# One-hots counted column by column, and the first node step and the lists between the pieces of the second sort, in a two-layer graph kernel

## The chip, the cores and the metric

The kernel runs on one core of a Trainium2 chip. The metric is the device time of one execution in microseconds (us). Eleven executions of the kernel before gave a median of 9892.93 us, from 9871.71 to 9947.75 us. Traces and profiles show a single execution. The engines are PE (matrix multiply), DVE (elementwise work), ACT (copies and functions), POOL (which issues the indirect transfers) and SP (which issues the plain transfers).

## The reference, cut to what matters

Two graph layers on 12,500 nodes of 128 features and 200,000 edges `src -> dst`. The first layer is a graph convolution with two sparse products, the second is attention with eight heads whose scores get a bias from a 128-wide attribute of every edge. Shortened:

```
mask = (src != dst); deg = segment_sum(mask, dst) + 1; dinv = deg ** -0.5
edge_w = dinv[src] * dinv[dst] * mask
spmm(h) = segment_sum(h[src] * edge_w, dst) + h / deg
h = spmm(relu(bn(spmm(x @ W1 + b1))) @ W2 + b2)
x = layernorm(x + h)
q, k, v = x @ q_w.T + q_b, x @ k_w.T + k_b, x @ v_w.T + v_b     # 8 heads of 16
scores = (q[src] . k[dst]) / 4 + edge_attr @ eb_w.T + eb_b
attn = softmax of scores over the edges of one src
x = layernorm(x + segment_sum(attn * v[dst], src) @ out_w.T + out_b)
```

The edges come in the order of `dst`. For the sparse products the kernel needs them grouped by pairs of blocks (128 nodes are a block, and there are 98), for the attention grouped by `src`. It makes both groupings on the chip.

## The kernel before

The edges lie as 128 partitions x 1563 columns. The work goes through these stages, and the change touches the first five of them.

**First sort, counts and records.** `load_raw` brings in `src` and `dst`. `keys_by_src` and `keys_by_blocks` make two sets of sort keys (128 x 2048). `bitonic` (L436) is a generator of 185 pieces (186 with the store behind it): compare-and-exchange steps on DVE (L460, L458 with a change of sign), and 14 times a turn of the whole array through PE and ACT (`turned`, L463 to L476), after which the generator yields 3. Beside the first sort, `counts` (L226) counts edges for each pair of blocks: for 16 columns at a time (`CW`) it writes three one-hots per edge (block of `dst`, block of `src`, row in the block: 98, 98 and 128 wide) with three DVE comparisons of the whole chunk (L234), each of two broadcast operands, and multiplies them on PE (L239, one matmul per column, summed in PSUM). It yields 2 after each of its 98 chunks. `woven` alternates the two generators and lets a yield of n hold its own generator back until the other has made n steps. `records` is a third generator, with 395 steps: it loads the edge attributes, turns them (PE L749, ACT L751), multiplies them by the bias weights (PE L764), and every eighth step turns the result back (ACT L777, PE L780) for DVE to add the bias (L782) and SP to store (L795) a table `rec` of records in DRAM. One of its steps, every third time two, follows each step of the weave.

**Decode of the first sort.** `windows_s` and `windows_a` find where each block begins. POOL gathers the sorted keys in tiles (`windowed`), and `decode_s` takes them apart on DVE: the edge numbers `idx_s`, rows, masks and gates for the attention, the last two with waits for their own stores and loads.

**Second sort and lists.** `beside` puts twelve pieces of the second sort (`sort_a`) under the first wait of `decode_s` and runs the rest of the second sort behind it. `chunks_b` is a generator of 83 steps (the lists `idx_b`, `loc_b`): 68 of them are eight DVE comparisons (L406, one per column of the list, 128 wide, with a per-partition scalar) and eight small matmuls (L408), and nine bring the results into form (L414 to L424). One step of it follows each piece of the sort from the 21st on. Then `decode_a` gathers and takes apart the second sort.

**The filler.** `placed` (L813) is a generator of 106 steps. A step has POOL gather one group of 16 x 128 records (16 indirect transfers, L809) through four buffers, and SP store the group that was gathered two steps earlier (L824). There are 104 groups, so the last two steps only store. The filler is stepped every eighth piece of the second sort beyond the 40th (19 times), every fourth step of the first node step (7), every 16th step of the first spread (31), every third step of the second node step (9) and every 16th step of the second spread (31). What is left of it runs out in a loop of its own before the second sum.

**First node step, then spread and sum.** `nodes_1` (L1079) loads `x`, turns it (PE L850, ACT L852), multiplies by W1 (PE L864) and writes `h_all` on DVE (`send`, L1076 and L1077), 25 groups in a pipeline. `spread` (488 tiles: one-hot on DVE L1007, four matmuls L1016, ACT L1020, store by SP L1025) writes a message per edge slot, and `summed` (544 tiles: gather by POOL, one-hot L1047, matmuls L1055, DVE L1061) adds them up by destination. `nodes_2`, a second spread and sum and `nodes_3` follow, and then attention and the output step, which the change leaves alone.

Each engine works through its own list in the order in which the generators above issued the work (the order is written by hand), so a generator that is stepped earlier moves all that it issues, on every engine and on SP and POOL too.

Of the kernel before, what the change touches and what calls it, by code (L numbers as in the profile page):

```python
# [1 line left out]

# [14 lines left out]
P = 128  # L17
# [3 lines left out]
G = 4  # L21
# [5 lines left out]
CW = 16  # L27
# [38 lines left out]


def beside(a, b):

    for n in a:  # L70
        yield
        for _ in range(n or 0):
            if next(b, StopIteration) is StopIteration:
                break
            yield
    yield from b
# [3 lines left out]
def kernel(  # L80
# [145 lines left out]
    def counts(pool, hi_s, hi_d, row_d):  # L226

        w = 2 * NB + P
        for c0 in range(0, EC, CW):
            n = min(CW, EC - c0)  # L230
            oh = pool.tile([P, CW, w], BF16, name="count_oh", bufs=3)
            k = 0
            for val, m in ((hi_d, NB), (hi_s, NB), (row_d, P)):
                nc.vector.tensor_tensor(  # L234
                    oh[:, :n, k:k + m], val[:, c0:c0 + n].unsqueeze(2).to_broadcast([P, n, m]),
                    iota_bf[:, :m].unsqueeze(1).to_broadcast([P, n, m]), op=ALU.is_equal)
                k += m
            for c in range(n):
                nc.tensor.matmul(pair_ps[:NB], oh[:, c, :NB], oh[:, c, NB:],  # L239
                                 start=(c0 + c == 0), stop=(c0 + c == EC - 1))  # L240
            yield 2
# [62 lines left out]
    def windows_s(pool, cnt):  # L304

        tiles, _, end = in_tiles(pool, cnt, 7, "s")
        pst = past(pool, end, NT, "past_s")
        by_j = pst.rearrange("b (p j) -> b j p", j=TPP)
        got = begins(pool, cnt, tiles, P, lambda j: by_j[:NB, j, :], TPP, pst, iota_w, "s")
        blk_i = pool.tile([1, NT], I32, tag="row", name="blk_i", bufs=1)  # L310
        tile_blocks(pst, NT, blk_i)
        nc.sync.dma_start(blk_sd, blk_i)
        return got
# [122 lines left out]
    def bitonic(pool, key, nm, out_):  # L436
# [42 lines left out]
        for k in range(1, LOGN + 1):  # L479
# [12 lines left out]
            else:  # L492
                key = turned(key, None)
                yield 3
# [4 lines left out]
                yield 3  # L499
# [35 lines left out]
    def sort_a(key):  # L535

        got = []
        yield from bitonic(keyp, key, "d", got)
# [3 lines left out]
    def decode_a(pool, begin):  # L542
# [6 lines left out]
        s_i = pool.tile([P, w], I32, tag="dec0", name="s_a", bufs=1)  # L549
        nc.vector.tensor_scalar(s_i, ff, 7, P - 1, op0=ALU.logical_shift_right,  # L550
                                op1=ALU.bitwise_and)
        seq = pool.tile([P, JA, R, P], BF16, tag="dec1", name="seq_at", bufs=1)
# [13 lines left out]
        drop = pool.tile([P, w], F32, tag="dec0", name="drop_a", bufs=1)  # L566
# [44 lines left out]
    def sort_s(key):  # L611

        got = []
        yield from bitonic(keyp, key, "s", got)
# [3 lines left out]
    def decode_s(pool, begin, blk):  # L618
# [12 lines left out]
        g = pool.tile([P, KC], I32, tag="dec0", name="g_s", bufs=1)[:NG]  # L631
        nc.vector.tensor_scalar(g, f, 31, None, op0=ALU.arith_shift_right)
        nc.vector.tensor_tensor(g, g, f, op=ALU.bitwise_xor)
        top = pool.tile([P, KC], F32, tag="dec1", name="top_s", bufs=1)[:NG]
# [10 lines left out]
        e_i = pool.tile([P, KC], I32, tag="dec1", name="e_i", bufs=1)[:NG]  # L645
# [6 lines left out]
        r_i = pool.tile([P, KC], I32, tag="dec1", name="r_i", bufs=1)[:NG]  # L652
# [4 lines left out]
        nd = pool.tile([P, TPP, P], F32, tag="dec0", name="nd", bufs=1)  # L657
# [4 lines left out]
        seq = pool.tile([P, KC], BF16, tag="dec1", name="seq", bufs=1)[:NG]  # L662
# [3 lines left out]
        loc_s = pool.tile([P, NT], F32, tag="row", name="loc_st", bufs=1)  # L666
# [194 lines left out]
    def times(psp, xt, n, w):  # L861
        mp = psp.tile([P, G, D], F32, tag="mp", name="n_mp", bufs=3)
# [30 lines left out]


    with ExitStack() as pre:
        ep = pre.enter_context(tc.tile_pool(name="edges", bufs=1))
        idx_s = ep.tile([P, NT], I32, name="idx_s")
        idx_b = ep.tile([P, NTB], I32, name="idx_b")
        loc_a = ep.tile([P, NTA, R], F32, name="loc_a")
        loc_b = ep.tile([P, NTB, R], F32, name="loc_b")  # L900
        blk_a = ep.tile([1, NTA], I32, name="blk_a")
        blk_b = ep.tile([1, NTB], I32, name="blk_b")
        filler = placed(ep)
        with tc.tile_pool(name="keys", bufs=1) as keyp, \
                tc.tile_pool(name="recs", bufs=1) as rp, \
                tc.tile_pool(name="pp", bufs=1, space=bass.MemoryType.PSUM) as pp:
            pair = rp.tile([P, 2 * NB], F32, name="pair", bufs=1)
            raw_d = load_raw(rp, dst, "d")
            table = records(rp)
            step(table)  # L910
            with tc.tile_pool(name="count", bufs=1) as pool:
                his = [pool.tile([P, EC], BF16, name=n_) for n_ in ("hi_s", "hi_d", "row_d")]
# [13 lines left out]
                pair_ps = pp.tile([P, NB + P], F32, tag="ps", name="pair_ps", bufs=2)  # L926
                with tc.tile_pool(name="count_oh", bufs=1) as pool:
                    sort = woven(counts(pool, *his), sort_s(key_s))
                    n = 0
                    while step(sort):  # L930
                        n += 1
                        step(table, 1 if n % 3 else 2)
            with tc.tile_pool(name="decode", bufs=1) as pool:

                nc.scalar.copy(pair[:NB, :NB], pair_ps[:NB, :NB])
                deg_r = pool.tile([P, P], F32, name="deg_r")
                nc.vector.tensor_scalar(deg_r[:NB], pair_ps[:NB, NB:], 1.0, None, op0=ALU.add)
                tp = pp.tile([P, NB], F32, tag="tp", name="pair_t", bufs=3)
                nc.tensor.transpose(tp[:NB], pair[:NB, :NB], ident[:NB, :NB])
                pair_t = pool.tile([P, NB], F32, name="pair_t")  # L940
                nc.vector.tensor_copy(pair_t[:NB], tp[:NB])
                cnt = pool.tile([P, 1], F32, name="cnt")[:NB]
                nc.vector.tensor_reduce(cnt, pair_t[:NB], AX.X, ALU.add)
                tp = pp.tile([P, NB], F32, tag="tp", name="deg_t", bufs=3)
                nc.tensor.transpose(tp, deg_r[:NB], ident[:NB, :NB])
                nc.scalar.activation(dinv, tp, AF.Sqrt)
                nc.vector.reciprocal(dinv, dinv)
                iota_t = pool.tile([P, NT], F32, name="iota_t")
                nc.gpsimd.iota(iota_t, pattern=[[1, NT]], base=0, channel_multiplier=0,  # L949
                               allow_small_or_imprecise_dtypes=True)  # L950
                iota_w = pool.tile([P, TPP], F32, name="iota_w")
                nc.gpsimd.iota(iota_w, pattern=[[P, TPP]], base=0, channel_multiplier=KC,
                               allow_small_or_imprecise_dtypes=True)
                iota_a = pool.tile([P, JA], F32, name="iota_a")
                nc.gpsimd.iota(iota_a, pattern=[[P, JA]], base=0, channel_multiplier=1,
                               allow_small_or_imprecise_dtypes=True)
                nc.vector.tensor_scalar(iota_a, iota_a, float(SA), None, op0=ALU.mult)
                sort = beside(decode_s(pool, *windows_s(pool, cnt)), sort_a(key_d))
                begin_a, first_a = windows_a(pool, cnt)
                lists = chunks_b(pool, pair[:, :NB], pair_t, first_a)  # L960
                early, n = 0, 0
                while step(sort):
                    n += 1
                    step(table, 2)
                    if n > 20:
                        step(lists)
                    if n % 8 == 0 and n > 40:
                        early += 1
                        step(filler)
                while step(lists):  # L970
                    pass
                for _ in decode_a(pool, begin_a):
                    pass
                while step(table):
                    pass

# [4 lines left out]

        h_all = wp.tile([P, NB, D], F32, name="h_all")
# [90 lines left out]
        def send(mp, bias, b, n):  # L1073

            o = h_all[:, b:b + n, :]
            nc.vector.tensor_add(o, mp[:, :n, :], wide(bias, n))  # L1076
            nc.vector.tensor_mul(o, o, tall(dinv[:, b:b + n], n))  # L1077

        def nodes_1():  # L1079
            a, c, e = {}, {}, {}  # L1080

            def s0(i):
                a[i] = load_x(pool, *groups[i])

            def s1(i):
                c[i] = transposed(pool, pp, a.pop(i), groups[i][1])

            def s2(i):
                e[i] = times(pp, c.pop(i), groups[i][1], w1_s)

            def s3(i):
                send(e.pop(i), b1_r, *groups[i])

            yield from pipeline(len(groups), s0, s1, s2, s3)

# [56 lines left out]
        with_records(nodes_1(), 4)  # L1152
        with_records(spread(msg1, D + 1), 16)
# [3 lines left out]
        with_records(spread(msg2, D), 16)  # L1157
# [43 lines left out]
    def attention(wp, psp):  # L1201
# [191 lines left out]
        chain = None  # L1393
        for s in range(NQ + ADD):
# [24 lines left out]
            for gen in bulk:  # L1419
                for _ in gen:  # L1420
                    left -= 1
                    if chain is not None and not step(chain):
                        chain = None
            if chain is not None and left > 0 and not step(chain, left):
                chain = None
            if 0 <= i < NQ and i % QN == QN - 1:
                chain = maxima(i // QN)
                step(chain)
# [89 lines left out]
```

## Time and profile before

| what | value |
|---|---|
| median of 11 executions | 9892.93 us |
| the profiled execution's own time | 9889.83 us |
| its span, first to last instruction | 9888.0 us |
| mean granted PE clock | 0.747 |
| busy share PE, DVE, ACT, POOL | 62%, 58%, 21%, 45% |

Stages, as the first and last instruction of their lines bound them:

| stage | from, us | to, us |
|---|---|---|
| first sort, counts, records | 66 | 1215 |
| windows, decode of the first sort | 1215 | 1412 |
| second sort with lists | 1412 | 1980 |
| decode of the second sort | 1980 | 2012 |
| first node step | 2012 | 2195 |
| first spread, first sum | 2195 | 4242 |
| second node step | 4242 | 4553 |
| second spread | 4553 | 5711 |
| rest of the filler, start of the second sum | 5711 | 5868 |

In a group of instructions the profile gives the line, engine, operation, tile written and tiles read, shapes and count, and after the bars the busy time with the mean of one, and the idle time of the engine before them with what ended it. "issue" and "remote" stand for a wait whose releaser the profile does not know. A timeline row gives start, duration, engine, line and tiles, and in brackets the idle time before it; rows of one kind are drawn together with a count.

### The profile page before, as it was taken

The page shows a single profiled execution, that of the slowest core. Times are in us where ns is not written, and L with a number is a line of the kernel's source. Part 1 is how long each engine was busy: PE and PEld are TensorE (multiplying, and loading weights), DVE is VectorE, ACT ScalarE, POOL GpSimd, SP SyncE. Part 2 cuts the span into 40 slices and gives each one's busy share as a digit, 9 for nine tenths or more (in the row PEclk, how much of TensorE's full clock was granted, in tenths as well). Part 3 has the DMA queues.
Part 4 walks back from the last instruction along what each step waited for, and adds up shares of the span by engine and source line. Part 5 has one row for each costly group of instructions (what it writes and reads, how often), then busy time and mean ns, then how long its engine had stood idle before and what let it go on. Part 6 is the DMA issues. An engine that isn't in the chain of part 4 may idle for free.

```text
span 9888.0 us, 117573 instructions
## 1 busy us (share of the span) xinstructions
PE 6131.8 (62%) x32059; PEld 4692.6 (47%) x32059; DVE 5686.5 (58%) x11412; ACT 2077.8 (21%) x5494; POOL 4497.4 (45%) x4450
## 2 busy tenths in 40 slices
PE   5777713137666777716767637772566676766665
PEld 2444412125555577615555526662455555555554
DVE  8888769723223466624323325557566666666667
ACT  1222200002222200002222200001233333333332
POOL 0000068263333366672433367760556565565651
PEclk9998855557777799956777769996666766676765
DMA  3333320013333466712333336673333333333343
GB/s 86 93 91 91 96 71 6 2 44 112 113 109 112 137 179 178 174 21 74 117 108 115 115 77 178 178 168 106 119 107 108 110 108 110 107 108 110 108 108 73
DMA packets 570541, 1045.40 MB, mean 106 GB/s; under 512 B 131594, under 2 KB 294678, under 8 KB 557252
## 3 DMA queue, kind: packets, MB, share of 16 engines
q0 software_dynamic: 220992, 514.28, 21.0%
q1 hardware_dynamic: 348928, 523.60, 16.0%
q8 instruction: 297, 4.87, 0.2%
q14 instruction: 324, 2.65, 0.1%
HBM read 722.51 MB, written 314.96 MB: 105 GB/s over the span
## 4 chain that ended last, share of the span: by engine, by line
PE 32%; DVE 12%; another core or an unknown queue 11%; issue 11%; POOL 4%; DMA 2%; DVEq 1%; ACT 1%; ACTq 0%; POOLq 0%; SPq 0%
PE ps L1055 12%; PE ex L1016 9%; POOL kvg L809 3%; PE qe L1259 3%; PE bc L1002 3%; PE ps L1379 2%; DVE acc L1381 2%; DVE kvg L1358 1%; DVE kvg L1269 1%; DMA got<-msg,idx_b 1%; DMA kvg<-kv,rec_in 1%; PE n_mp L864 1%; DVEq L889 1%; DVE oht L1248 1%
## 5 line engine op out<-in xcount | busy, mean ns | idle before, releaser
L809 POOL DMA_INDIRECT placed<-rec,idx_s x1664 | 1717.9, 1032 | 1838.2 <-DMA rec_s<-placed 1304.5
L809 POOL DMA_INDIRECT kvg<-kv,rec_in x1664 | 1636.9, 984 | 1391.3 <-PE ps L1379 574.9
L1016 PE MATMUL ex<-h_all,oht 128*128 x7808 | 1353.7, 326 | 731.4 <-DVE oht L1007 464.2
L1007 DVE TENSOR_SCALAR oht<-bc,iota_col 128x512 f32<-128x512 f32 x976 | 722.9, 750 | 1656.6 <-remote 805.1
L1016 PEld LDWEIGHTS ex<-h_all,oht 128*128 128x128 f32 x7808 | 1150.5, 226 | 1004.5 <-issue 687.4
L1055 PE MATMUL ps<-got,oh 128*128 128x128 f32 x8704 | 1232.1, 299 | 564.2 <-DVE acc L1061 275.8
L1055 PEld LDWEIGHTS ps<-got,oh 128*128 128x128 f32 x8704 | 1125.2, 207 | 671.1 <-DVE acc L1061 332.0
L809 POOL DMA_INDIRECT got<-msg,idx_b x1088 | 1115.9, 1026 | 559.8 <-PE ps L1055 234.6
L1379 PE MATMUL ps<-kvg,oh 128*128 128x136 f32 x3328 | 801.6, 384 | 462.1 <-DVE acc L1381 271.8
L1020 ACT COPY et<-ex 128x512 f32<-128x512 f32 x976 | 567.3, 587 | 1779.9 <-issue 745.1
L1259 PE MATMUL qe<-q_all,oht 128*128 x3328 | 905.6, 411 | 50.3 <-DVE oht L1248 11.2
L1379 PEld LDWEIGHTS ps<-kvg,oh 128*128 128x128 f32 x3328 | 647.5, 267 | 546.0 <-DVE acc L1381 319.7
L1259 PEld LDWEIGHTS qe<-q_all,oht 128*128 128x128 f32 x3328 | 690.4, 259 | 267.2 <-issue 194.7
L1047 DVE TENSOR_TENSOR oh<-loc_b,iota_row 128x512 f32<-128x512 f32 x1088 | 757.3, 696 | 18.9
L1381 DVE TENSOR_TENSOR acc<-acc,ps 128x136 f32 x1248 | 366.1, 293 | 607.5 <-PE ps L1379 198.8
L1061 DVE TENSOR_TENSOR acc<-acc,ps 128x128 f32 x1088 | 308.2, 283 | 697.4 <-PE ps L1055 466.2
L1351 ACT ACTIVATE sq<-iota_row,loc_s 128x128 f32<-128x128 f32 x1664 | 529.8, 388 | 10.3
L949 POOL IOTA iota_t<- 128x1664 f32 x1 | 1.5, 1530 | 1164.5 <-PE pair_ps L239 1164.5
L764 PE MATMUL bp<-attr_t,ebw_at 128*64 128x512 f32 x782 | 442.7, 649 | 0.1
L751 ACT COPY attr_t<-tp 128x512 f32<-128x512 f32 x391 | 229.1, 586 | 956.3 <-PE tp L749 953.7
L1002 PE MATMUL bc<-seq_l,ones_bf 1*128 1x512 bf16 x976 | 422.5, 434 | 0.0
L460 DVE TENSOR_TENSOR key_d<-key_d 128x512 f32<-128x512 f32 (+1 forms) x468 | 397.9, 903 | 38.1 <-ACT key_d L475 30.9
(361 smaller groups left out, 6842.7 us busy)
## 6 DMA issues: line engine op xcount, KB each, us to landing
msg<-et SPq DMA_DIRECT2D x488, 258.0 KB
msg<-et SPq DMA_DIRECT2D x488, 256.0 KB
attr<-in_edge_attr_dram SPq DMA_DIRECT2D x97, 896.0 KB
seq_in<-row_seq SPq DMA_DIRECT2D x104, 512.0 KB
placed<-rec,idx_s POOLq DMA_INDIRECT x1664
kvg<-kv,rec_in POOLq DMA_INDIRECT x1664
got<-msg,idx_b POOLq DMA_INDIRECT x1088
masks<-mk SPq DMA_DIRECT2D x16, 832.0 KB
```

The costliest lines, as they stand in the source:

```text
L764: nc.tensor.matmul(sums[i // RQ][:RQ * H].rearrange("h g p -> h (g p)"), ebw_at[:, (RQ - 1 - r) * H:(2 * RQ - 1 - r) * H], tts.pop(i).rear ...
L809: nc.gpsimd.indirect_dma_start(out=out_, out_offset=None, in_=table, in_offset=bass.IndirectOffsetOnAxis(ap=idx, axis=0))
L1002: nc.tensor.matmul(bcs[t], ones_bf[:1, :], seqs[t // SQ][:, t % SQ * SA:][:, :SA], start=True, stop=True)
L1007: nc.vector.tensor_scalar(ohs[t].rearrange("p k c -> p (k c)"), bcs.pop(t), iota_col, None, op0=ALU.is_equal)
L1016: nc.tensor.matmul(exs[t][:, k, :], o[:, k, :], hb, start=True, stop=True)
L1020: nc.scalar.copy(ets[t][:, :, :D], exs.pop(t))
L1047: nc.vector.tensor_tensor(oh[t], loc_b[:, t, :].unsqueeze(2).to_broadcast([P, R, P]), iota_row.unsqueeze(1).to_broadcast([P, R, P]), op=AL ...
L1055: nc.tensor.matmul(ps[t], o[:, k, :], x_[:, k, :D], start=(k == 0), stop=(k == R - 1))
L1259: nc.tensor.matmul(qe[:, k, :], o[:, c * P:(c + 1) * P], qb, start=True, stop=True)
L1351: nc.scalar.activation(sq[:, k, :], iota_row, AF.Square, bias=loc_s[:, t:t + 1])
L1379: nc.tensor.matmul(ps, o[:, k, :], t[:, k, P:], start=True, stop=True)
L1381: nc.vector.tensor_add(*adds)
```

## The change

- `counts` works on chunks of 8 columns, and instead of three comparisons per chunk it makes three per column: the row of numbers (`iota_bf`, bf16) against one column's value as a per-partition scalar. The values `hi_s`, `hi_d`, `row_d` are fp32 now. It yields 1 after each of its 196 chunks.
- After a turn the first sort yields 2, the second 4 (before, 3). The function `beside` is gone.
- The records get one step per step of the weave, and what is left of them runs out at the end of the first sort, so that their buffers are freed there.
- `decode_s` starts with its gather, then `windows_a` and four steps of the lists are issued, then the rest of `decode_s`, the second sort and `decode_a` in one chain. Beside this chain run the lists and behind them the first node step, which has moved here with one idle stage after its load: four steps after each turn of the second sort, else one for every third piece.
- The filler is stepped at every seventh piece of that chain beyond the 16th (26 times), every 14th step of the first spread and every 12th of the second.
- Temporary tiles share buffers with the keys of the first sort (`spare`) and with one another.

The diff, cut to its core:

```diff
-CW = 16
+CW = 8
...
-            for val, m in ((hi_d, NB), (hi_s, NB), (row_d, P)):
-                nc.vector.tensor_tensor(
-                    oh[:, :n, k:k + m], val[:, c0:c0 + n].unsqueeze(2).to_broadcast([P, n, m]),
-                    iota_bf[:, :m].unsqueeze(1).to_broadcast([P, n, m]), op=ALU.is_equal)
-                k += m
+            for c in range(n):
+                k = 0
+                for val, m in ((hi_d, NB), (hi_s, NB), (row_d, P)):
+                    nc.vector.tensor_scalar(oh[:, c, k:k + m], iota_bf[:, :m],
+                                            val[:, c0 + c:c0 + c + 1], None, op0=ALU.is_equal)
+                    k += m
...
-            yield 2
+            yield 1
...
-                yield 3
+                yield gap
...
-        yield from bitonic(keyp, key, "d", got)
+        yield from bitonic(keyp, key, "d", 4, got)
...
-        yield from bitonic(keyp, key, "s", got)
+        yield from bitonic(keyp, key, "s", 2, got)
...
+    def nodes_1(pool, psp):
...
+        def s2(i):
+            e[i] = times(psp, c.pop(i), groups[i][1], w1_s, 2)
...
+        yield from pipeline(len(groups), s0, lambda i: None, s1, s2, s3)
...
-                    n = 0
                     while step(sort):
-                        n += 1
-                        step(table, 1 if n % 3 else 2)
+                        step(table)
+                while step(table):
+                    pass
...
-                sort = beside(decode_s(pool, *windows_s(pool, cnt)), sort_a(key_d))
-                begin_a, first_a = windows_a(pool, cnt)
-                lists = chunks_b(pool, pair[:, :NB], pair_t, first_a)
-                early, n = 0, 0
-                while step(sort):
-                    n += 1
-                    step(table, 2)
-                    if n > 20:
-                        step(lists)
-                    if n % 8 == 0 and n > 40:
-                        early += 1
-                        step(filler)
...
+            decode = decode_s(pool, *windows_s(pool, cnt))
+            step(decode)
+            nc.vector.tensor_scalar(iota_a, iota_a, float(SA), None, op0=ALU.mult)
+            begin_a, first_a = windows_a(pool, cnt)
+            lists = chunks_b(pool, pair, pair_t, first_a)
+            step(lists, 4)
+
+            beside_ = chain(lists, nodes_1(first_nodes, pp))
+            n = 0
+            for gap in chain(decode, sort_a(key_d), decode_a(pool, begin_a)):
+                n += 1
+                step(beside_, gap or (n % 3 == 0))
+                if n > 16 and n % 7 == 0:
+                    step(filler)
+            while step(beside_):
+                pass
...
-        with_records(nodes_1(), 4)
-        with_records(spread(msg1, D + 1), 16)
+        with_records(spread(msg1, D + 1), 14)
...
-        with_records(spread(msg2, D), 16)
+        with_records(spread(msg2, D), 12)
```

## The prediction

> **What bounds the kernel now.** I read the stages first: busy time of each engine between the first and last instructions of a stage, then granted PE clock, share of the transfer engines, GB/s.
>
> ```profile
> core 0: us, PE busy (x) PEld busy (x) DVE busy (x) ACT busy (x) POOL busy (x), PEclk, DMA share, GB/s
> 66.00:1215.00 1149.00, 888.83 (x4243) 475.51 (x4243) 987.18 (x885) 273.39 (x481) 1.71 (x3) 0.92 0.32 92
> ...
> 1412.00:1980.00 568.00, 135.99 (x788) 100.26 (x787) 487.62 (x1058) 47.10 (x68) 328.26 (x234) 0.53 0.05 4
> ...
> 2012.00:2195.00 183.00, 65.50 (x295) 55.91 (x296) 33.90 (x50) 14.92 (x26) 104.60 (x111) 0.56 0.19 41
> 2195.00:3403.00 1208.00, 829.21 (x4392) 622.04 (x4390) 362.83 (x491) 327.96 (x976) 459.78 (x488) 0.74 0.35 112
> ...
> 4553.00:5711.00 1158.00, 803.36 (x4282) 603.04 (x4281) 351.97 (x476) 275.20 (x478) 449.06 (x477) 0.75 0.34 113
> 5711.00:5868.00 157.00, 7.88 (x32) 7.05 (x32) 13.96 (x8) 0.05 (x1) 109.51 (x106) 0.51 0.19 32
> ```
>
> The two sorts are DVE's (987 of 1149 us, 488 of 568). In the first node step and the spreads no engine is full: something makes them wait. So DVE work counts in full in the sorts, and in the other stages I look for what they wait for.
>
> Next, DVE's waits, first sort and second sort:
>
> ```profile
> DVE rec_o L782 <- PE tp L780: 107.3, 43, 7.4
> DVE key_s L458 <- ACT key_s L473: 26.8, 4, 9.2
> DVE key_s L460 <- ACT key_s L475: 23.1, 3, 9.6
> ```
>
> ```profile
> DVE key_d L460 <- ACT key_d L475: 30.9, 4, 12.6
> ```
>
> In the first sort DVE idles 158 us (its gaps, total, longest in the columns), 107 at the adding of the bias, about 50 after turns. The second loses some 66 us, nearly all after turns.
>
> Last, the timeline of the first node step and of the first spread:
>
> ```profile
> 2042.19 2.08 PE L864 MATMUL n_mp<-w_s,n_t 128*128 128x128 f32 x8 [15.52 <-issue]
> ...
> 2061.85 0.69 DVE L1076 TENSOR_TENSOR h_all<-n_mp,b_r 128x512 f32<-128x512 f32 x1 [27.29 <-remote]
> ```
>
> ```profile
> 2591.88 0.75 DVE L1007 TENSOR_SCALAR oht<-bc,iota_col 128x512 f32<-128x512 f32 x1 [0.65 <-PE bc L1002]
> 2593.29 0.75 DVE L1007 TENSOR_SCALAR oht<-bc,iota_col 128x512 f32<-128x512 f32 x1 [0.65 <-PE ex L1016]
> ...
> 2602.94 0.75 DVE L1007 TENSOR_SCALAR oht<-bc,iota_col 128x512 f32<-128x512 f32 x1 [4.96 <-remote]
> 2614.20 0.75 DVE L1007 TENSOR_SCALAR oht<-bc,iota_col 128x512 f32<-128x512 f32 x1 [10.51 <-remote]
> ```
>
> The matmuls begun at 2042.2 were followed by DVE only at 2061.9: while POOL gathers for the filler, PE's results reach others up to some 17 us late. The spread runs at 1.40 us a tile (2591.88 to 2593.29) until the next gathers start at 2593, then at 5 to 11 us. So each filler costs the spread time: 1208 us less 488 x 1.40 = 683 leaves 525 for 31 fillers, **16.9 us each**; second spread (1158 - 683) / 31 = 15.3.
>
> **The change, part by part**, against the profiled execution's 9889.8 us (3 us under the median of 9892.9; span 9888.0).
>
> *One-hots.* Now, per 16 columns:
>
> ```profile
> 300.23 1.78 DVE L234 TENSOR_TENSOR count_oh<-hi_d,iota_bf 128x1568 bf16<-128x1568 bf16 x1
> 301.93 1.78 DVE L234 TENSOR_TENSOR count_oh<-hi_s,iota_bf 128x1568 bf16<-128x1568 bf16 x1
> 303.63 2.28 DVE L234 TENSOR_TENSOR count_oh<-row_d,iota_bf 128x2048 bf16<-128x2048 bf16 x1
> 305.84 5.02 DVE L460 TENSOR_TENSOR key_s<-key_s 128x512 f32<-128x512 f32 x8
> ```
>
> From start to start 305.84 - 300.23 = 5.61 us, 0.351 a column, x 1563 = 548 us. After, 3 x 1563 = 4689 small instructions. The nearest row is the list comparison, bf16, 128 wide, with a per-partition scalar:
>
> ```profile
> L406 DVE TENSOR_SCALAR step<-iota_bf,base_t x544: 240/248/489, 1433.4 to 1722.2; 98x128 bf16<-98x128 bf16 x182
> ```
>
> ```profile
> 1433.44 0.41 DVE L406 TENSOR_SCALAR step<-iota_bf,base_t 98x128 bf16<-98x128 bf16 x2
> ```
>
> Two take 0.41 us, one 0.248: the second starts 0.162 after the first. Width counts for little: an 8-wide one with such a scalar (L1340) lasts 220 ns, this one 248, so 28 ns for 120 more and 7 less for 98, 0.155. A column: 2 x 0.155 + 0.162 = 0.472; x 1563 = 738 us. **+190**. Bounds: 0.134 each (8 wide: 0.162 - 0.028) gives 628, +80; the full 0.248 without overlap 1163, +615. I take the row, which is the same operation back to back.
> The Trainium skill ("VectorE: DVE Perf Modes", the section on the TRN2 errata) charges 58 cycles plus the width over 4, by an estimate 86 and 94 ns, 415 us in all, and the whole sum would then be 323 us lower; it says too that many small tiles pay the fixed part per tile, which speaks against the change, and the row's 162 ns sides with that.
>
> *DVE's idle time in the first sort.* After the smaller chunks PE has 8 matmuls to catch up on, not 16 (1.7 us at L239), and each can follow its own column. In the new order every turn is followed by 48 or 72 small comparisons (7.5 us or more) where the waits were 5 to 10: gone. The 49 waits at L782 (about 2 us) fall to about 1: PE has now 12.5 us per 16 columns for what took it 9. 158 to some 58: **-100** (bounds 0 and -158). What is late next is DVE itself.
>
> *End of the records.* 10 of 395 steps are left, some 6 turns of 1.6 us on PE, nothing beside them: **+10** (0 to +25).
>
> *First node step.* Its stage goes, 183 us less 8 for the first spread's first load: -175. Its 25 groups come back in the second sort: SP's loads (three buffers ahead, behind the filler's stores), PE's turns and matmuls, ACT's copies, and 2 x 0.61 us on DVE. The order has 13 sends singly between compares (1.3 us, all else under DVE): 17 us. Four each stand behind three turns, in which DVE now waits about 4.4 us: there send, matmul, turn and copy chain at 3.65 us a group at this clock (sends at 2062.58 and after, 2064.73 to 2068.38 on ACT), three such links behind the turn, some 11 us more than now; with PE's results held by gathers 10 us a group as at 2016 to 2064, 30 more. The gathers run through the sort (26 groups x 16 at about 1.7 us, 707 us), so I take 18 each, 54. **-175 + 71 = -104** (bounds -125, -50). Queued behind a waiting DVE is the sort itself.
> The skill's page "SBUF - State Buffer" (the section on its two separate sides) says that only DVE and GpSimd block each other and PE never waits; the 17 us above speak against it, and by the rule alone this term would be some 20 us better.
>
> *Lists and decode.* Four list steps fill the wait for the decode's gather, which had twelve pieces of the sort: these come back later, the list steps save as much; with four list steps behind each of nine turns DVE still waits for PE's turn first. **-8** (-25 to +20).
>
> *Filler.* 104 groups: 19 + 7 + 31 + 9 + 31 + 7 left over; now 26 + 0 + 35 + 9 + 34 + 0. First spread +4 x 16.9 = **+68**; second +3 x 15.3 = **+46**; the rest's loop goes: the second sum started 157 us after the spread where the first needs 12, **-145**. So moving the filler is nearly a null: a group costs as much under a spread as alone (7 x 20 us). Seven more in the second sort ride under DVE, POOL being idle there from 1811 to 1984.
>
> **Sum:** 190 - 100 + 10 - 104 - 8 + 68 + 46 - 145 = **-43**: 9846.8, say **9847 us**.
>
> **Rivals.**
> 1. *The small comparisons are dearer and it is slower.* Each instruction's price x enters 4689 times; the sum is zero at x = 0.157 + 43 / 4689 = 0.167 us, and 0.2% slower (about what a measurement tells from no change, 20 us) above 0.171. At 0.18, if 98 wide costs more than by the rows, 844 us: +106 on the sum, +63, 9953. For: nothing in the trace is 98 wide and this kind; single L406 last up to 0.489. Against: L406 is wider.
> 2. *The gaps of the second sort swallow the node step.* PE's results are held at every link: 3 x 30 more instead of 3 x 18, and the list gaps 5 us each: +36 + 45 on the sum, 9928. For: the waits of 12.6 us after turns occur only while POOL gathers. Against: DVE busy slows the gathers, and with 1.7 us each the holds are rarer.
> 3. *More is hidden.* All 158 us of idle time go and the sends fit: -58 - 40 on the sum, 9749.
> 4. *The filler's move pays.* If a filler costs the spread less when tighter (say 10 us): -7 x 6 = 42 more, 9805.
>
> **Numbers.** Forecast (-43, give or take 40) 0.43, rival 1 0.22, rival 2 0.13, rival 3 0.14, rival 4 0.08. Faster by over 0.2% (below 9873): 0.43 x 0.7 + 0.14 + 0.08 = 0.52; within: 0.43 x 0.25 + 0.13 x 0.4 = 0.16; slower 0.32. The range takes in rivals 1 and 3: 9745 to 9970; the full 0.248 of the small ones (+425) stays outside.
>
> **What would show it.** One-hots: L225 in rows of 24, 24 of them in 3.8 us; stage one some 105 us longer. No waits after turns there, about 1 us at the bias. The second sort with 4 sends behind three turns and waits of 10 to 30 us there; the first spread beginning right after the second decode. Spreads of about 1276 and 1204 us, and the second sum starting at once. Wrong if a small comparison starts over 0.171 us after the one before it, or if PE, not DVE, ends the waits of the first sort.

## The result and the profile after

The changed kernel takes **10027.02 us** (median of 8, 10001.5 to 10036.84), the kernel before 9894.37 (31 runs): ratio **1.0127**, 95% interval 1.0111 to 1.0142. I had forecast 9847, and a range that ended at 9970. The profiled execution took 9990.8 us (span 9989.0), 101 us more by span than that of before. It is the quickest one of its kernel, so some 32 us of the 133 between the medians are in no profile here.

The stages of the changed kernel, in the columns shown for before:

```profile
core 0: us, PE busy (x) PEld busy (x) DVE busy (x) ACT busy (x) POOL busy (x), PEclk, DMA share, GB/s
66.00:1330.00 1264.00, 1050.22 (x4328) 477.67 (x4328) 1180.91 (x5302) 281.77 (x497) 1.69 (x3) 0.93 0.29 87
...
1474.00:2066.00 592.00, 118.33 (x702) 85.66 (x703) 416.26 (x998) 24.04 (x39) 279.51 (x256) 0.51 0.05 6
2066.00:2291.00 225.00, 76.11 (x381) 66.54 (x379) 157.32 (x168) 29.20 (x47) 115.83 (x96) 0.61 0.17 42
2291.00:3594.00 1303.00, 874.55 (x4390) 656.25 (x4389) 361.25 (x489) 326.61 (x976) 533.46 (x564) 0.71 0.34 104
...
4701.00:5952.00 1251.00, 864.74 (x4391) 648.82 (x4389) 361.49 (x491) 280.21 (x488) 484.21 (x512) 0.72 0.33 107
5952.00:6783.00 831.00, 595.98 (x4351) 538.10 (x4351) 484.18 (x1088) 0.00 (x0) 583.20 (x544) 0.95 0.64 174
```

The first sort is 106 us longer, as I had worked out. The leftover filler is gone: the second sum follows the second spread at once. Both spreads are longer (1208 and 1179 before). The surprise is in the second row, the second sort while the lists last: of 592 us DVE works 416. Its waits from 1660 to 1840, and from 1840 to 2066 (total, number, longest):

```profile
DVE step L396 <- remote: 66.6, 28, 3.2
DVE step L396 <- issue: 59.1, 10, 35.9
DVE step L396 <- PE list_ps L398: 9.5, 9, 1.8
DVE step L396 <- PE tp L459: 3.1, 1, 3.1
```

```profile
DVE step L396 <- PE list_ps L398: 23.1, 8, 3.2
DVE step L396 <- remote: 3.7, 2, 1.9
```

L396 is the list comparison. In the first stretch it waits 138 us, in the second, which is longer and does more, 27. The timeline of DVE in the one (with the matmul of one comparison on PE) and in the other:

```profile
1776.59 0.25 DVE L396 TENSOR_SCALAR step<-iota_bf,base_t 98x128 bf16<-98x128 bf16 x1 [2.55 <-remote]
1776.90 0.19 PE L398 MATMUL list_ps<-steps,step 98*128 98x6 bf16 x1 [2.61 <-issue]
1779.39 0.25 DVE L396 TENSOR_SCALAR step<-iota_bf,base_t 98x128 bf16<-98x128 bf16 x1 [2.55 <-remote]
1782.19 0.26 DVE L396 TENSOR_SCALAR step<-iota_bf,base_t 98x128 bf16<-98x128 bf16 x1 [2.55 <-remote]
```

```profile
1883.15 0.73 DVE L396 TENSOR_SCALAR step<-iota_bf,base_t 98x128 bf16<-98x128 bf16 x4
1887.10 4.64 DVE L396 TENSOR_SCALAR step<-iota_bf,base_t 98x128 bf16<-98x128 bf16 x28 [3.21 <-PE list_ps L398]
```

After each turn the change puts four list steps, 32 comparisons in a row, and their output has four buffers (`step`, `bufs=4`): from the fifth on, each waits until PE has read one four before it. At 1776 each wait is 2.55 us. At 1887, after a first wait of 3.21, the remaining 28 run through in 4.64 us. Between the two lies this: POOL gathered for the filler until 1833.8 and then stood still until 2082.6, because a store of the filler was queued on SP behind loads of `x`:

```profile
1756.24 322.68 SPq L828 DMA_DIRECT2D x_in<-in_x_dram  x7
2079.22 0.34 SPq L814 DMA_DIRECT2D rec_s<-placed  x1
```

The two turns under gathers held up the sort by 44 us (1671.2 to 1715.1) and 116 (1719.1 to 1835.6); at seven turns behind them L396 waits about 3 us once. These seven fell into POOL's standstill, so the loss measured here is not what nine turns under gathers would cost.

Gathers alone do not make these waits. Just before the first of the two turns eight comparisons ran through beside gathers, and in the kernel before all 544 ran beside them, eight at a time, with 10 us of waits (the last two lines):

```profile
1665.17 1.46 DVE L396 TENSOR_SCALAR step<-iota_bf,base_t 98x128 bf16<-98x128 bf16 x8
1677.01 0.42 DVE L396 TENSOR_SCALAR step<-iota_bf,base_t 98x128 bf16<-98x128 bf16 x2 [0.85 <-PE list_ps L398]
```

```profile
DVE step L406 <- PE tp L469: 5.8, 2, 3.1
DVE step L406 <- PE list_ps L408: 4.4, 2, 3.1
```

The waits begin behind a turn and grow there unevenly, from 0.85 us at 1677 to 2.55 at 1703. What else it takes besides gathers (the many short PE results in a row, or gathers that no work of DVE spaces out) no run here separates.

Nor do the four buffers make all of the 138 us. One wait alone is 36 us, and ahead of it ACT's copies of the turn were late as well, though PE's last transposes had ended at 1728.1:

```profile
1726.98 1.11 PE L459 MATMUL tp<-ident,key_d 128*128 128x128 f32 x4 [4.96 <-ACT key_d L465]
1756.99 0.69 ACT L465 ACTIVATE key_d<-tp,signs 128x512 f32<-128x512 f32 x1 [11.21 <-remote]
1759.79 0.25 DVE L396 TENSOR_SCALAR step<-iota_bf,base_t 98x128 bf16<-98x128 bf16 x1 [35.88 <-issue]
```

### The profile page after: what moved, and what is told of

It is laid out like the page before. It is cut to its first block, busy times and chain, and to the rows that moved or that the text cites. A ratio compares the mean times of both kernels' runs of the same rounds, so it can differ in the third digit from the quotient of the medians.

```text
span 9989.0 us, 121833 instructions
## 1 busy us (share of the span) xinstructions
PE 6327.7 (63%) x32059; PEld 4717.1 (47%) x32059; DVE 5874.5 (59%) x15807; ACT 2074.3 (21%) x5494; POOL 4466.3 (45%) x4450
## 4 chain that ended last, share of the span: by engine, by line
PE 33%; DVE 12%; another core or an unknown queue 11%; issue 10%; POOL 4%; DMA 3%; DVEq 1%; ACT 1%; SPq 0%; POOLq 0%; ACTq 0%
PE ps L1071 12%; PE ex L1032 11%; POOL kvg L799 4%; PE bc L1018 3%; PE qe L1251 3%; PE ps L1371 2%; DVE acc L1373 2%; DMA got<-msg,idx_b 1%; DVE kvg L1350 1%; DMA kvg<-kv,rec_in 1%; DVE kvg L1261 1%; PE n_mp L854 1%; DVEq L879 1%; DVE acc L1077 1%
## 5 line engine op out<-in xcount | busy, mean ns | idle before, releaser
L799 POOL DMA_INDIRECT placed<-rec,idx_s x1664 | 1657.0, 996 | 1889.8 <-DMA rec_s<-placed 1359.5
L1032 PE MATMUL ex<-h_all,oht 128*128 x7808 | 1425.8, 339 | 812.1 <-DVE oht L1023 570.4
L1032 PEld LDWEIGHTS ex<-h_all,oht 128*128 128x128 f32 x7808 | 1215.1, 238 | 1099.2 <-issue 712.2
L799 POOL DMA_INDIRECT got<-msg,idx_b x1088 | 1142.0, 1050 | 692.4 <-PE ps L1071 211.8
L1071 PEld LDWEIGHTS ps<-got,oh 128*128 128x128 f32 x8704 | 1105.2, 204 | 556.1 <-DVE acc L1077 345.8
L229 PE MATMUL pair_ps<-count_oh 128*98 128x226 bf16 x1563 | 329.3, 262 | 227.2 <-DVE count_oh L225 219.2
L754 PE MATMUL bp<-attr_t,ebw_at 128*64 128x512 f32 x782 | 472.0, 689 | 0.0
```

The costliest lines, as they stand in the source:

```text
L754: nc.tensor.matmul(sums[i // RQ][:RQ * H].rearrange("h g p -> h (g p)"), ebw_at[:, (RQ - 1 - r) * H:(2 * RQ - 1 - r) * H], tts.pop(i).rear ...
L799: nc.gpsimd.indirect_dma_start(out=out_, out_offset=None, in_=table, in_offset=bass.IndirectOffsetOnAxis(ap=idx, axis=0))
L1032: nc.tensor.matmul(exs[t][:, k, :], o[:, k, :], hb, start=True, stop=True)
L1071: nc.tensor.matmul(ps[t], o[:, k, :], x_[:, k, :D], start=(k == 0), stop=(k == R - 1))
```

## The experiments

All runs below were on five chips on which the kernel before takes 8135 to 8157 us, 18% less than where the result was measured. Each ratio is to the kernel before on the same chip.

Theory **L**: the unforeseen loss is the list comparisons behind turns, which wait for PE one by one. **H**: they do so because POOL's gathers hold up PE's results. Rivals: **O**, the one-hots cost more than the first sort shows; **N**, the node step between the pieces costs the time; **F**, the filler's new steps do.

### Old one-hots (two runs)

```diff
-CW = 8
+CW = 16
...
-                    nc.vector.tensor_scalar(oh[:, c, k:k + m], iota_bf[:, :m],
-                                            val[:, c0 + c:c0 + c + 1], None, op0=ALU.is_equal)
+                nc.vector.tensor_tensor(
+                    oh[:, :n, k:k + m], val[:, c0:c0 + n].unsqueeze(2).to_broadcast([P, n, m]),
+                    iota_bf[:, :m].unsqueeze(1).to_broadcast([P, n, m]), op=ALU.is_equal)
...
-            yield 1
+            yield 2
```

> The changed kernel with the counting of the kernel before (chunks of 16 columns, three comparisons of the whole chunk, bf16 values, weave 2 and 3); the rest of the change stays. In the two traces the first sort with records grew by 106 us (start of the windows 1224.7 to 1330.8). Theory L (the loss that I had not foreseen lies in the second sort, where 32 list comparisons behind each of two turns wait one by one for PE): the first sort goes back to about 1225, 106 us less, and everything behind it stays as in the changed kernel: about 9920, ratio to the kernel before 1.003. Rival O (the small comparisons are the cause of the whole loss, in ways that show later too): at or below the kernel before less 20, 9875 or under. Rival S (the first sort's gain from filled idle time was the point, so that the old one-hots in the new weave are no better): 10010 or more.

Measured: 1.0142 (1.0125 to 1.0159). It tells nothing of the one-hots: a weave with fewer pieces steps the records less often, and they ran on alone for some 200 us after the sort (to 1404 us). The next run also steps the records as before (`step(table, 1 if n % 3 else 2)`).

> The changed kernel with the counting of the kernel before and with the records stepped as before (every third time two steps), so that they end with the sort; the run before this one left 110 record steps to the end and is no test. First sort to the start of the windows: 1225 to 1250 in place of 1331, so 80 to 106 us under the changed kernel of this call, whatever the chip. By the rival that the idle time filled makes up for the small comparisons: within 30 us of it.

Measured: **0.9957** (0.9944 to 0.997), 85 us under the changed kernel on the same chip; the windows begin at 1250.5 instead of 1334.9. So the one-hots cost what the first sort shows and no more, and the rest of the change gains on these chips. O has fallen.

### One-hots alone, on the kernel before

> The kernel before with the per-column one-hots alone (8 columns to a chunk, fp32 values, a yield of 1); weave of the records, second sort, node step and filler as before. By the two traces the first sort's part of the change cost 106 us, of which about 10 are the records' end that is missing here: +90 to +115, about 9994, ratio 1.009 to 1.012. If the end of the records or the gap of 2 instead of 3 is what costs, and the one-hots are made up for by the filled idle time, under +40. By the sum of my prediction (+190 for the comparisons, -100 for idle time) +90.

Measured: **1.0092** (1.0075 to 1.0109), 81 us; in the trace the windows begin 100 us later than in the trace of before from such a chip (1326.5 against 1226.8).

### Both kernels unchanged, and the filler's steps

> The kernel before, unchanged, for its stages on the chip of these runs. In the four runs so far its median was 8147 us, not 9894, and the spreads of the four kernels took 1.40 us a tile while POOL gathered. If gathers do not hold up PE here either: first spread 686 us (not 1207), first node step some 90 us (not 183), second node step 141 (not 290), total near 8147. If they do, the stages of the first trace.

> The changed kernel, unchanged. Theory L+H (32 list comparisons behind a turn wait for PE, and only because PE's results come late while POOL gathers): on a chip where the gathers do not hold PE the waits at L396 (162 us in the changed kernel's trace) are under 40, and the time is that of the run with 32 buffers, within 15 us: 8150 to 8185, ratio 1.001 to 1.005. If four buffers are too few in any case, 1.008 or more with over 80 us of waits at L396. On a chip where they do hold PE: 1.011 to 1.014 as measured. Rival W (the change loses the same share everywhere, by the one-hots): 1.0127 also here.

Measured: before 8150.8 (one execution). **Changed 1.0054** (1.0037 to 1.0071), just above the 1.001 to 1.005 that I expected. Waits at L396 in the second sort:

```profile
DVE step L396 <- PE list_ps L398: 25.2, 9, 3.2
```

25 us, not 162, with the same code and buffers and with gathers beside most of the comparisons. And the spreads, kernel before (two rows), then changed kernel (two rows):

```profile
2097.00:2799.00 702.00, 690.66 (x4391) 520.26 (x4389) 377.02 (x491) 333.18 (x976) 500.65 (x531) 0.99 0.69 194
...
3663.00:4363.00 700.00, 689.50 (x4391) 519.32 (x4389) 376.32 (x489) 285.66 (x488) 519.48 (x539) 0.99 0.60 192
```

```profile
2131.00:2838.00 707.00, 687.23 (x4392) 517.50 (x4390) 377.15 (x491) 333.44 (x976) 534.26 (x567) 0.99 0.69 193
...
3725.00:4553.00 828.00, 754.15 (x4392) 565.85 (x4390) 376.80 (x490) 286.06 (x488) 547.96 (x574) 0.90 0.54 164
```

About 700 us where the first traces have 1200, with as many gathers. In the changed kernel's first spread here DVE keeps its 1.40 us a tile while POOL gathers every 1.25 us:

```profile
2399.35 0.75 DVE L1023 TENSOR_SCALAR oht<-bc,iota_col 128x512 f32<-128x512 f32 x1 [0.65 <-PE bc L1018]
...
2399.64 0.94 POOL L799 DMA_INDIRECT placed<-rec,idx_s  x1 [0.30 <-issue]
...
2400.76 0.75 DVE L1023 TENSOR_SCALAR oht<-bc,iota_col 128x512 f32<-128x512 f32 x1 [0.66 <-PE bc L1018]
...
2400.89 0.94 POOL L799 DMA_INDIRECT placed<-rec,idx_s  x1 [0.30 <-issue]
```

So gathers of the same length and pace go with late results of PE where the result was measured, and on these chips they do not. One stage does lose here, the second spread (828 against 700). The filler every 16th tile again:

```diff
-        with_records(spread(msg1, D + 1), 14)
+        with_records(spread(msg1, D + 1), 16)
...
-        with_records(spread(msg2, D), 12)
+        with_records(spread(msg2, D), 16)
```

> The changed kernel with the filler stepped every 16th tile in both spreads (as before) in place of 14 and 12; seven groups then run out alone ahead of the second sum. Where gathers hold PE: spreads some 70 and 46 us shorter, 120 to 145 longer behind the second spread, net 0 to +40. Where they do not: the first spread is the same (686), the second 813 against 687 of the kernel with the old filler steps, so 126 less, and 110 to 130 for the leftover gathers: net -20 to +20.

Measured: **1.0027** (1.0017 to 1.0037), 25 us under the changed kernel. The second spread fell by 126 us, the leftover gathers cost some 115 of it. SP's own waits in the second spread, first the changed kernel (up to 4441 us, where its last gather ends), then this run:

```profile
SPq L814 <- DMA placed<-rec,idx_s: 270.4, 54, 7.8
SPq L1041 <- ACT et L1036: 170.4, 174, 4.7
```

```profile
SPq L1041 <- ACT et L1036: 430.3, 481, 4.7
SPq L814 <- DMA placed<-rec,idx_s: 4.4, 7, 2.2
```

L814 stores a filler group, L1041 a message tile, and SP works through one list in order:

```profile
4011.96 3.92 SPq L1041 DMA_DIRECT2D msg<-et  x3
4022.35 0.32 SPq L814 DMA_DIRECT2D rec_s<-placed  x1
4022.77 0.38 SPq L1041 DMA_DIRECT2D msg<-et  x1
```

16 gathers take 16 x 1.25 = 20.0 us. Twelve tiles take 12 x 1.40 = 16.8, so the store of a group comes up before its gathers are done, and the messages queue behind it; sixteen tiles take 22.4. F is a real cost, but on these chips of another kind than the one I had priced.

### Lists: more buffers (three runs), one step at a time, no gathers

```diff
-                st = pool.tile([P, P], BF16, name="step", bufs=4)
+                st = pool.tile([P, P], BF16, name="step", bufs=32)
```

> The changed kernel with 32 buffers in place of 4 for the list comparisons' output, so that the 32 comparisons behind a turn can all be written before PE has read the first. Theory L: the idle time of DVE at L396 in the second sort (162 us) falls to under 60; what stays is the wait for the turn itself (PE's matmuls, ACT's four copies), which PE's late results stretch while POOL gathers: the sort (1474 to 2256) becomes 60 to 130 us shorter, the time 9900 to 9970. Rival N (the first node step between the pieces is what costs, not the lists): under 20 us less, 10007 or more. Rival H (hand-overs from PE are late whatever the buffers, and the wait only moves from L396 to the compare behind the turn): also under 20 us less, but with L396's waits gone and equal ones at L450 and L448.

> The changed kernel with 32 buffers for the list comparisons, once more. In the first traces (kernel before 9894 us) the waits at L396 were 162 us; in the changed kernel's run at 8207 us they were 25, and the spreads ran at 1.40 us a tile under gathers. Where gathers hold PE (kernel before near 9894): waits at L396 under 60, the sort 60 to 130 us shorter, ratio 1.000 to 1.007 against 1.0127. If the wait only moves to the compare behind the turn: 1.010 to 1.014. Where they do not hold it (kernel before near 8150): 1.000 to 1.003 again.

> The changed kernel with 32 buffers for the list comparisons a third time, to meet a chip on which gathers hold PE's results (kernel before near 9894). There: waits at L396 under 60 of 162, the sort 60 to 130 us shorter, ratio 1.000 to 1.007; if the wait only moves, 1.010 to 1.014. Where they do not hold it: 1.000 to 1.004 as twice before.

Measured: 1.0016 (1.0002 to 1.0029), 1.0024 (1.0013 to 1.0035) and 1.0047 (1.0024 to 1.0069), with the changed kernel at 1.0054. No wait at L396 is left in any of the three traces, and no new one at the turns: the sort takes 589 to 590 us where the changed kernel takes 617. So the four buffers cost the sort 27 us even where PE's results are not held, and N does not explain these. In the whole time the gain is less sure: the third interval takes in the changed kernel's 1.0054. None of the runs met a place where PE's results are held, so what 32 buffers bring there was not measured. The 36 us wait would hardly have gone, since the last copy of that turn itself ended only at 1757.7.

```diff
-            beside_ = chain(lists, nodes_1(first_nodes, pp))
+            beside_ = nodes_1(first_nodes, pp)
...
-                step(beside_, gap or (n % 3 == 0))
+                if not step(lists):
+                    step(beside_, gap or (n % 3 == 0))
```

> The changed kernel with the lists stepped once behind each piece of the sort, as in the kernel before, and the node step only from when the lists are done (then as in the change, four behind a turn). Theory L: in the kernel before such single list steps cost DVE about 16 us of waits over the whole sort, so most of the 162 us at L396 go; some 12 to 35 us come back where a turn now stands with one list step behind it while POOL gathers (12.6 and 9.3 us in the kernel before). Net 90 to 140 us less: 9890 to 9940, ratio 0.999 to 1.005. Rival N (the node step costs the time): no gain or a loss, because the node step gets fewer turns: 10010 to 10060.

Measured: 1.0077 (1.0059 to 1.0094), an interval that overlaps with that of the change. By stages it is worse: from the windows to the first spread 808 us, 791 in the changed kernel. The waits at L396 fell to 4 us, but eight turns stood open again (4.1 to 4.6 us each), and the filler's gathers stood ahead of the second decode's gather on POOL until 2115 us, 15 us after the sort. Where PE's results are not held, then, four list steps behind a turn cover it better than one: 38 us of waits at turns and lists here, 29 in the changed kernel.

```diff
-                if n > 16 and n % 7 == 0:
-                    step(filler)
```

> The changed kernel with no filler step in the second sort; its 26 groups run out alone ahead of the second sum (26 x 20 us more there), so that only the second sort's stage is read. Theory H (late results of PE are the gathers' doing): on a chip where gathers hold PE, the waits at L396 fall from 162 to under 40 and the sort (1474 to 2256 in the first trace, 782 us) to 600 to 650. On one where they do not, the stage stays at 617 us and the waits at L396 at 25: four buffers behind a turn cost 3 us each, gathers or not.

Measured: 8594.8 us in all, with 21 groups run out alone (not 26, the second spread took in five more), and in the second sort 611 us (617 with gathers) and

```profile
DVE step L396 <- PE list_ps L398: 26.7, 9, 3.2
```

On this chip the gathers cost the second sort 6 us at most, and none at L396. H is read from the two stretches of one trace: no run took the gathers away where they hold PE's results, so what they do there to the 162 us is argued and not tested.

### Gathers one at a time

```diff
+                nc.gpsimd.tensor_copy(tick, ohs[t][:, 0, :1])
+                step(filler)                 # a step is now one gather, in every tile of a spread
```

> The changed kernel with the filler's gathers spread out: in both spreads one gather a tile, behind a one-column copy by POOL of that tile's one-hot, so that POOL waits for DVE before each; elsewhere 16 at a time as before, and some eight groups run out ahead of the second sum. Where gathers hold PE: if it is POOL working back to back that holds PE's results, the spreads (1303 and 1251 us) fall to 700 to 900 each, ratio 0.90 to 0.96; if every gather has its price however spaced (17 us for 16), 488 of them cost 518, the spreads 1200 and the ratio 1.00 to 1.02. Where they do not hold PE: the first spread stays near 690, the second falls from 814 to 690 to 760 (a gather every 1.41 us where POOL takes 1.26), and eight groups alone cost 160: ratio 1.005 to 1.015; if copy and gather together take more than a tile, both spreads stretch to 750 or more.

Measured: 1.0122 (1.0105 to 1.0139). First spread 686.5 us, second 727.8, eight groups alone some 154: the case without a hold. Whether spacing helps where there is one was not measured.

### Put together

Old one-hots, filler every 16th tile, 32 buffers:

> The changed kernel with three things put back or eased: the counting of the kernel before (with its records weave), the filler every 16th tile in both spreads, and 32 buffers for the list comparisons. On a chip where gathers do not hold PE, one at a time against the kernel before: -36 us for the old one-hots in the new order, 25 less for the filler (1.0054 to 1.0027), 31 less for the buffers (1.0054 to 1.0016). If they add up: 8150 - 92, some 8060, ratio 0.987 to 0.990. If the list waits were hidden behind the turn anyway, 0.991 to 0.994. On a chip like that of the first traces (median before near 9894), where I put the list waits at 137 us and the one-hots at 106: 0.985 to 0.995.

Measured: **0.9911** (0.9894 to 0.9927), 79 us where the three alone add up to 92. Then also:

```diff
+                    if i in (5, 7):          # ahead of the decode's two waits
+                        for _ in range(8):
+                            yield next(order)    # pieces of the second sort
...
-        while step(filler):
-            pass
         for _ in summed(msg2, D):
             pass
-        for _ in nodes_3():
-            pass
+        with_records(nodes_3(), 3)
+        while step(filler):
+            pass
```

> The run above with two further edits: eight pieces of the second sort under each of the two waits of the first decode (30.5 and 38.3 us of idle DVE in the changed kernel), and the leftover filler under the third node step (157 us in which POOL does nothing) instead of alone ahead of the second sum. Where gathers do not hold PE: 60 less for the waits, 111 less for the leftover loop (883 us of second sum with it, 772 without it) and up to 30 back for the third node step, so some 130 to 165 us under the run above: 7895 to 7930, ratio 0.968 to 0.973. If the stores behind the third node step's loads hold it back (the queue of SP is served in order, and a store waits for its gathers, 20 us a group), only 60 to 100 less. Where gathers hold PE: the third node step grows by 100 or more, and the gain is 60 to 100.

> The version with old one-hots, filler every 16th tile, 32 buffers, pieces of the second sort under the waits of the first decode, and the leftover filler under the third node step, once more, for its time where gathers hold PE: the third node step 100 or more longer there, the rest as put down: ratio 0.975 to 0.990. Where they do not: 0.969 to 0.972 again.

Measured: **0.9702** (0.9685 to 0.9718) and 0.9688 (0.9668 to 0.9707): 249 us under the kernel before, and the third node step is as long as ever (156 us). This version beats both kernels, on these chips.

## Why the prediction was wrong, step by step

Stages by their first and last DVE instructions, changed less before, in us; "other" is the pair of unchanged kernels on one of the other chips:

| step | predicted | where the result was measured | other |
|---|---|---|---|
| one-hots, idle time, end of records | +100 | +106 | +108 |
| first node step moved | -104 | -103 | -26 |
| lists, decode | -8 | **+92** | -48 |
| first spread | +68 | +96 | +5 |
| first sum, second node step | 0 | -22 | +23 |
| second spread | +46 | +72 | +127 |
| leftover filler, second sum | -145 | -131 | -121 |
| rest | 0 | -9 | -2 |
| sum | -43 | +101 | +66 |

Of the 144 us between my sum and the profile, the lists are 100 and the two spreads 54; the rest is 10 the other way.

*One-hots: right.* 0.157 us from one to the next was the price I took, from a row 98 partitions high, and it is what they cost:

```profile
300.56 0.24 DVE L225 TENSOR_SCALAR count_oh<-iota_bf,hi_d 128x98 bf16<-128x98 bf16 x1
300.71 0.24 DVE L225 TENSOR_SCALAR count_oh<-iota_bf,hi_s 128x98 bf16<-128x98 bf16 x1
300.87 0.24 DVE L225 TENSOR_SCALAR count_oh<-iota_bf,row_d 128x128 bf16<-128x128 bf16 x1
```

Width does not show: 98 and 128 wide start 0.15 to 0.16 us after one another. So Rival 1, dearer comparisons, did not come about. I quoted from the Trainium skill ("VectorE: DVE Perf Modes", the section on the TRN2 errata) the fixed 58 cycles; the same section says that this under-predicts the duration of one operation and that the measured fixed term is about 150 cycles. By an estimate from that term, its clock and the width over 4, one comparison lasts 182 or 190 ns. The trace has 240 ns, and 157 from start to start, the figure that the sum needs.

*Idle time in the first sort: right.* The last compare ended at 1214.9 and ends at 1308.3, +93: 188 for the one-hots less 95. DVE's waits fell from 159 us to 68 up to there. Turns show none; the bias kept more than I gave it (61 us of 107, where I had some 49).

*First node step: right in size.* 183 us are gone, where I had 175, and 80 come back, where I had 71: DVE waits 46 us at the sends (eight waits of 3 to 9 us and three under 2, where I had three of 18) and works 34 on them. That the sum came within 1 us is luck, since two misses of 8 and 9 us cancel.

*Lists and decode: this step failed.* I wrote "with four list steps behind each of nine turns DVE still waits for PE's turn first", and left it at -8. That first wait was there, 3 us at seven turns. What I put at nothing, without a reason, were the 32 comparisons behind it: through four buffers they are 28 hand-overs to PE, and I did not look whether they could run. I had the price of a late hand-over in hand and applied it to the node step alone. In the whole second sort the compares behind turns waited 57 us before and 4 after, as the change meant; L396 waited 10 us before and 165 after. Rival 2 came nearest (it charged 45 us to the lists, "5 us each").

That L396 waits for PE and that this is the loss, the trace shows. How much of it is the four buffers and how much the late results of the turn itself stays open, since no run was made in that place.

*Filler: the mechanism held where I had seen it, the sizes were low.* 564 gathers fell into the first spread and not 35 x 16 = 560, but before it had been 488, not 31 x 16 = 496: 4.75 groups more, not 4, and (1303 - 683) / 35.25 = 17.6 us each, where it had been 525 / 30.5 = 17.2. My stage of the second spread began 21 us late (it runs from 4532, 1179 us and not 1158), so a group had cost 16.5 us there and not 15.3; with two groups more it costs 17.8. Rival 4, a lower price when tighter, went the other way. On the other chips a group costs the spreads nearly nothing until it takes POOL longer than the tiles between two steps: +5 us at 20.0 against 14 x 1.40 = 19.6, +127 at 20.0 against 16.8. Rival 3, more hidden, did not come about: most of the bias waits stayed.

*What I could not have read.* That PE's results come late while POOL gathers belongs to where the kernel ran: five other chips do not show it (1.40 us a tile under gathers). My prediction set it against the skill's page "SBUF — State Buffer". That page ("SBUF: two separate sides") says of the engines' access to SBUF that PE and ACT never wait for anyone. The trace does not speak against that sentence: beside the gathers too, PE begins the matmul 0.31 us after its comparison began (1776.59 and 1776.90). Late is the hand-over of its result to DVE and ACT. Why that is so, and whether it lies in the chip, no run here shows.

## What to carry to other kernels

Work moved into a wait covers it only if it can run there. Count its own hand-overs and buffers: 32 pieces through 4 buffers can be 28 waits for the other engine, at whatever a hand-over costs at that place (here nearly nothing, or some 2.5 us). A store that waits for a slow producer holds all that is queued behind it, so step such a producer no oftener than it can finish: 20.0 us of gathers every 16.8 us cost 126 us, every 22.4 nothing. And a price read from one trace can belong to the place where it was taken: repeat the unchanged kernel elsewhere before building on it.

## What the runs showed that I had not expected

- The kernel before takes 9894 us in one place and 8135 to 8157 on five other chips. Its first spread took 1204 us there and 689 here, its first node step 183 and 84, its second 290 and 141: the stages with gathers beside PE's hand-overs. The gathers start 1.25 us apart in both.
- A comparison of a bf16 row against a per-partition scalar starts every 0.157 us whether it writes 98 or 128 columns.
- In one trace, 100 us apart, the same list comparisons behind a turn start every 0.16 us without gathers and every 2.80 us beside them, while eight between two compares start every 0.17 us beside gathers as well. The gathers beside the long waits are not longer for it (0.94 or 0.95 us, as on the other chips).
